# A decoder layer on one core: where the routed tiles' next rows are loaded and turned, and which buffers the shared down weights use

## Chip, cores and metric

The kernel runs on one core of one Trainium2 chip. The metric is device time in microseconds; the kernel before took 1041.7 us (median of three runs, 1040.75 to 1043.2).

## The reference

One decoder layer on `x` of 8 sequences of 112 tokens (896 tokens, width 512, fp32), each part with a layer norm ahead of it and a residual sum behind it: causal attention with 16 heads of 128; cross attention with 32 heads of 16 to a context of 375 rows per sequence; and a mixture of experts. All that the change touches is in the last part:

```python
probs = softmax(x @ gate_w.T)                      # 8 experts, the best 2 of each token
routing_weights, selected = top_k(probs, 2)        # normed to a sum of 1
out = (silu(x @ shared_gate.T) * (x @ shared_up.T)) @ shared_down.T          # 704 wide
y[e] = (silu(x @ expert_gate[e].T) * (x @ expert_up[e].T)) @ expert_down[e].T  # 352 wide
out = out + sum over the token's two experts of weight * y[e]
```

## The kernel before

The first two thirds of the kernel (attention and cross attention) are the same before and after. The expert part begins with the shared gate and up projections (`shared_chunk`, L645) and the routing (`route`). Routing gives every pair of token and expert a slot. The slots of one expert stand together, in units of 64 slots, and two units make a tile of 128 slots: 18 tiles (`NS`), 36 units. GpSimd scatters the normed token rows into `slots` in DRAM (L807).

**The routed loop** (L956) goes over tiles j = 0 to 17 and one round more, as a pipeline over three steps of three tiles. In round j:

- `fetch(j+1)` (L835 to L844): SyncE loads the next tile's 128 rows from `slots` into `xt` (two buffers). TensorE transposes them in four 128x128 blocks into PSUM (`xt_t`, L841), ScalarE copies these to `xT` (L843).
- `gate_up(j, ...)` (L868): gate and up of tile j, in two halves of two chunks each of the 512 inputs. The two units of a tile use the two halves of TensorE's columns: unit 0 reads its expert's weights in place from `wex` at a register's offset, unit 1 reads a copy (`second`), which VectorE makes (`copy_second`, L831). So each matmul is 128 rows by 64 columns, and two run side by side.
- Between the two halves, `turn_hidden` (L885) transposes the hidden rows of tile j-1 in three blocks (`h_t`, L889), and VectorE copies them to `hT` (L890, L891).
- `gated(gu)` (L878): ScalarE's Silu (L880) and VectorE's product (L882) make the hidden rows of tile j.
- `down(j-1, ...)` (L894): six matmuls per tile, again two side by side (`y`, L898), a copy by ScalarE (L902) and a write to `routed` in DRAM from SyncE (L903).
- `load_down(j+1)` (L846): SyncE loads the down weights of the next tile's two units, each 256 rows (`wed_a`) and 96 rows (`wed_b`) of 512.

**Buffers of the down weights** (L948 and L949): the pool `weights` has three buffers of four 128x512 slices, `thirds`. Three units hold slices 0 to 2 of one buffer each, a fourth unit is pieced together from slice 3 of all three. Even tiles use buffers 0 and 1, odd tiles buffer 2 and the pieced one. So the last tile, 17, reads slice 3 of buffers 0 and 1.

**After the loop**, `wsd0` and `wsd1`, three slices each of the shared down weights, are loaded into the same pool (L978 to L982). GpSimd gathers every token's two routed rows (`add_routed`, L909), and VectorE adds them to the residual (L915). `finish` (L917) multiplies the shared hidden rows by the shared down weights on TensorE (`ys`, L924), two token tiles at a time in four groups, VectorE adds (L930), SyncE writes out (L931).

What sets the order: each engine works through its own instructions in the order in which the scheduler of the tile framework put them, which is close to the order of the code but not the same. DMAs are started by the engine named in the code (`nc.sync`, `nc.scalar`, `nc.gpsimd`) when their turn comes there, and wait in that engine's order for what they depend on. A tile of a pool that takes the place of an older one waits until all reads of the older one, in whichever slice, are done.

Of the kernel before, what the change touches and what calls it, by code (L numbers as in the profile page):

```python
# [15 lines left out]
F32 = mybir.dt.float32  # L16
# [5 lines left out]
P = 128  # L22
B, S, D = 8, 112, 512
# [20 lines left out]
NS = (NU + 1) // 2  # L44
# [32 lines left out]
def decoder_layer(  # L77
    ctx: ExitStack, tc: tile.TileContext, x, ctxT, wqk, wv_all, wo, wx, wgate, wsgu, wsd, wegu, wed_a, wed_b, consts, out
):
    nc = tc.nc  # L80
# [6 lines left out]
    wpool = ctx.enter_context(tc.tile_pool(name="weights", bufs=3))  # L87
# [26 lines left out]
    slots = dpool.tile([NS * P, D], F32, name="slots")  # L114
    routed = dpool.tile([NS * P, D], F32, name="routed")

    def psum(pool, name):
        return pool.tile([P, 512], F32, tag=pool.name, name=name)
# [53 lines left out]
    with ExitStack() as sa:  # L172
# [106 lines left out]
        for g in range(NG):  # L279
# [11 lines left out]
            if g == 0:  # L291
                first_weights = load.ins
                with tc.issue_after(first_weights):
                    nc.sync.dma_start(out=gw, in_=wgate)
                    nc.sync.dma_start(
                        out=slots.rearrange("(j p) d -> p j d", p=P),
                        in_=zeros[:, None, :].to_broadcast([P, NS, D]),
# [326 lines left out]
    with ExitStack() as ff:  # L624
# [4 lines left out]
        tp = ff.enter_context(tc.tile_pool(name="slot", bufs=2))  # L629
# [194 lines left out]
        def second(j, c):  # L824
            return stand[(j * ND + c) % len(stand)]

        def copy_second(j, chunks):
            if j not in moved:
                moved[j] = nc.vector.value_load(expert[:1, 2 * j + 1 : 2 * j + 2], min_val=0, max_val=E - 1)
            for c in chunks:  # L830
                nc.vector.tensor_copy(  # L831
                    second(j, c), wex[:, bass.ds(moved[j], 1), c, :].rearrange("p o f -> p (o f)")
                )

        def fetch(j):  # L835

            xt = tp.tile([P, D], F32, tag="xt", name="xt")
            nc.sync.dma_start(out=xt, in_=slots[j * P : (j + 1) * P, :])
            pt = psum(mm, "xt_t")
            for c in range(ND):  # L840
                nc.tensor.transpose(pt[:, c * P : (c + 1) * P], xt[:, c * P : (c + 1) * P], ident)  # L841
            xT = tp.tile([P, ND, P], F32, tag="xT", name="xT")
            nc.scalar.copy(xT, pt.rearrange("p (c s) -> p c s", c=ND))  # L843
            return xT  # L844

        def load_down(j):  # L846

            wd = down_w[2 * (j % 2) : 2 * (j % 2) + 2]
            for u in range(2):
                e = nc.sync.value_load(expert[:1, 2 * j + u : 2 * j + u + 1], min_val=0, max_val=E - 1)  # L850
                if u == 0 or j % 2 == 0:
                    w = wd[u]
                    nc.sync.dma_start(out=w[:, 0:2, :], in_=wed_a[bass.ds(e, 1)].rearrange("o p c d -> (o p) c d"))
                    nc.sync.dma_start(
                        out=w[: FCH[2][1], 2, :], in_=wed_b[bass.ds(e, 1)].rearrange("o p d -> (o p) d")
                    )
                    wd[u] = [w[:, i, :] for i in range(3)]
                else:
                    for i in range(2):
                        nc.sync.dma_start(  # L860
                            out=wd[u][i], in_=wed_a[bass.ds(e, 1), :, i].rearrange("o p d -> (o p) d")
                        )
                    nc.sync.dma_start(
                        out=wd[u][2][: FCH[2][1]], in_=wed_b[bass.ds(e, 1)].rearrange("o p d -> (o p) d")
                    )
            return wd

        def gate_up(j, e, xT, gu, chunks):  # L868
            for c in chunks:
                for k in range(2):  # L870
                    cols = slice(k * FF, (k + 1) * FF)
                    for n, w in (
                        (halves[0], wex[:, bass.ds(e, 1), c, cols].rearrange("p o f -> p (o f)")),
                        (halves[1], second(j, c)[:, cols]),
                    ):
                        nc.tensor.matmul(gu[k][n, :FF], xT[:, c, n], w, start=(c == 0), stop=(c == ND - 1))  # L876

        def gated(gu):  # L878
            g = tp.tile([P, FF], F32, tag="sg", name="sg")
            nc.scalar.activation(g, gu[0][:, :FF], AF.Silu)  # L880
            h = tp.tile([P, FF], F32, tag="sh", name="sh")
            nc.vector.tensor_tensor(h, g, gu[1][:, :FF], ALU.mult)  # L882
            return h

        def turn_hidden(h):  # L885
            pt = psum(mm, "h_t")
            hT = tp.tile([P, 3, P], F32, tag="hT", name="hT")
            for i, (f0, fn) in enumerate(FCH):
                nc.tensor.transpose(pt[:fn, i * P : (i + 1) * P], h[:, f0 : f0 + fn], ident)  # L889
            nc.vector.tensor_copy(hT[:, :2, :], pt[:, : 2 * P].rearrange("p (c s) -> p c s", c=2))  # L890
            nc.vector.tensor_copy(hT[: FCH[2][1], 2, :], pt[: FCH[2][1], 2 * P : 3 * P])  # L891
            return hT

        def down(j, hT, wd):  # L894
            ps = psum(mm, "y")
            for i, (_, fn) in enumerate(FCH):
                for n, w in zip(halves, wd):
                    nc.tensor.matmul(  # L898
                        ps[n, :], hT[:fn, i, n], w[i][:fn], start=(i == 0), stop=(i == len(FCH) - 1)
                    )  # L900
            y = tp.tile([P, D], F32, tag="y", name="y")
            nc.scalar.copy(y, ps)  # L902
            nc.sync.dma_start(out=routed[j * P : (j + 1) * P, :], in_=y)  # L903
# [44 lines left out]
        thirds = [wpool.tile([P, 4, 512], F32, tag="w", name=f"wd{i}") for i in range(3)]  # L948
        down_w = [*thirds, [t[:, 3, :] for t in thirds]]  # L949
        moved = {}  # L950
        copy_second(0, (0, 1))
        ready = {0: fetch(0)}
        wds = {0: load_down(0)}
        copy_second(0, (2, 3))
        h = {}
        for j in range(NS + 1):  # L956
            if j + 1 < NS:
                ready[j + 1] = fetch(j + 1)
            if j < NS:
                gu = [psum(sc, "gate"), psum(sc, "up")]  # L960
                e = nc.tensor.value_load(expert[:1, 2 * j : 2 * j + 1], min_val=0, max_val=E - 1)
                gate_up(j, e, ready[j], gu, (0, 1))
            if j + 1 < NS:
                copy_second(j + 1, (0, 1))
            if j >= 1:
                hT = turn_hidden(h.pop(j - 1))
            if j < NS:
                gate_up(j, e, ready[j], gu, (2, 3))
                if j + 1 < NS:
                    copy_second(j + 1, (2,))  # L970
                h[j] = gated(gu)
                if j + 1 < NS:
                    copy_second(j + 1, (3,))
            if j >= 1:
                down(j - 1, hT, wds.pop(j - 1))
            if j + 1 < NS:
                wds[j + 1] = load_down(j + 1)
        wsd_t = []  # L978
        for i in range(2):
            w = wpool.tile([P, 4, 512], F32, tag="w", name=f"wsd{i}")  # L980
            nc.sync.dma_start(out=w[:, :3, :], in_=wsd[:, 3 * i : 3 * i + 3, :])
            wsd_t.append(w)  # L982
        pairs = ((0, 4), (1, 5), (2, 6), (3,))
        for tiles in pairs:
            for t in tiles:
# [79 lines left out]
```

## Time and profile before

| What | Value |
|---|---|
| median of three runs | 1041.7 us (1040.75 to 1043.2) |
| profiled execution: its own time, its span | 1046.2 us, 1044.4 us |
| mean granted TensorE clock in that span | 0.991 |
| routed loop, from its first transposes to the last `y` | about 839.9 to 999.8 us of the span |
| `gate` and `up` (L876), copies included | 144 + 144 matmuls each on `wex`, 459 to 471 ns |
| `y` (L898) | 216, 592 ns |
| turned rows `xt_t` (L841), hidden rows `h_t` (L889) | 72 and 54, 284 and 291 ns |
| `ys` (L924) | 84, 644 ns |
| loads of rows `xt` (SyncE) | 18 of 256 KB, 5.3 us to landing |
| loads of shared down weights (SyncE) | 2 of 768 KB, 4.4 and 6.3 us to landing |

Durations of single matmuls overlap, for they are pipelined: the distance of their starts is what a matmul costs. The chain of waits gives that better; its lines hold a start, a length, an engine, the name of what was written, the line of the kernel and a count. Every fp32 matmul appears as two records, and one in which two units run side by side as four.

### The profile page before, as it was taken

Reading aid. Unit: us, or ns where it says so; the run is one execution under the profiler, and the core shown is the slowest. Engines: PE = TensorE matmul, PEld = TensorE weight load, DVE = VectorE, ACT = ScalarE, POOL = GpSimd, SP = SyncE. Lnnn points to the kernel's source line nnn. Section 1 sums busy time; section 2 is a strip of 40 time slices with the busy share of each in tenths; the row PEclk is TensorE's granted clock in tenths of the full one; section 3 lists DMA queues with packets and bytes.
Section 4 is the critical chain, followed back from the end, with each engine's and each line's share of the span. In section 5 each row is a group of like instructions: output and inputs, shape, how many; then the busy total and the mean of one; then the engine's idle time right before and its main releaser. Section 6 shows DMA issues by size and latency. Waiting matters only on the chain.

```text
span 1044.4 us, 14683 instructions
## 1 busy us (share of the span) xinstructions
PE 1020.3 (98%) x5760; PEld 540.1 (52%) x5760; DVE 381.8 (37%) x744; ACT 277.4 (27%) x516; POOL 201.3 (19%) x223
## 2 busy tenths in 40 slices
PE   5999999999999999999999999999999989999988
PEld 3556555655565455645555555556665544444433
DVE  3345234522453244654223332242224133333223
ACT  2122011201120013123545554565532011111100
POOL 3241044103410221132100111011053200000041
PEclk9999999999999999999999999999989999999989
DMA  9421002101210120001000000001158247777664
GB/s 347 178 85 46 24 18 83 47 0 41 82 48 1 41 82 8 1 1 41 30 31 31 1 31 30 32 1 41 42 226 323 93 143 226 228 226 230 209 194 121
DMA packets 31092, 95.66 MB, mean 92 GB/s; under 512 B 3888, under 2 KB 5808, under 8 KB 27440
## 3 DMA queue, kind: packets, MB, share of 16 engines
q1 hardware_dynamic: 28272, 86.31, 24.7%
q0 software_dynamic: 2320, 7.63, 2.3%
q8 instruction: 46, 0.75, 0.3%
q10 hardware_dynamic: 432, 0.79, 0.2%
q14 instruction: 22, 0.18, 0.1%
HBM read 78.85 MB, written 14.94 MB: 90 GB/s over the span
## 4 chain that ended last, share of the span: by engine, by line
PE 92%; issue 3%; DVE 2%; DMA 2%; POOL 1%; ACT 0%; SPq 0%; DVEq 0%; POOLq 0%; ACTq 0%
PE qk L256 15%; PE o L343 9%; PE v L333 9%; PE xv L435 8%; PE k L423 8%; PE gu L645 6%; PE xs L511 5%; PE gate L876 4%; PE y L898 4%; PE pv L536 4%; PE up L876 4%; PE ys L924 4%; PE z L221 2%; PE s L186 2%; PE qk L311 1%
## 5 line engine op out<-in xcount | busy, mean ns | idle before, releaser
L519 ACT ACTIVATE e<-xs 125x448 f32<-125x448 f32 x192 | 88.9, 549 | 51.5 <-PE xs L511 51.3
L333 PE MATMUL v<-w,xn 128*128 128x512 f32 x224 | 100.4, 594 | 0.0
L343 PE MATMUL o<-wo,zT 128*128 128x512 f32 x224 | 99.9, 594 | 0.0
L435 PE MATMUL xv<-wx,ctx 128*125 128x512 f32 x192 | 88.4, 603 | 0.0
L423 PE MATMUL k<-wx,ctx 128*125 128x512 f32 x192 | 87.6, 601 | 0.0
L256 PE MATMUL qk<-xc,wc 128*128 128x448 f32 x180 | 70.1, 539 | 0.0
L645 PE MATMUL gu<-xn,sw 128*128 128x448 f32 x176 | 67.5, 540 | 0.0
L343 PEld LDWEIGHTS o<-wo,zT 128*128 128x128 f32 x224 | 41.0, 190 | 44.1 <-issue 44.0
L333 PEld LDWEIGHTS v<-w,xn 128*128 128x128 f32 x224 | 40.7, 190 | 42.1 <-issue 41.1
L407 POOL TENSOR_TENSOR sq<-kraw 125x512 f32<-125x512 f32 x24 | 25.2, 1050 | 184.9 <-ACT kraw L405 184.9
L511 PE MATMUL xs<-qT,kT 32*125 32x224 f32 x768 | 55.4, 380 | 1.0 <-ACT e L519 1.0
L876 PE MATMUL gate<-wex,xT 128*64 x144 | 56.0, 471 | 0.3 <-ACT xT L843 0.3
L423 PEld LDWEIGHTS k<-wx,ctx 128*125 128x125 f32 x192 | 34.3, 187 | 40.1 <-issue 40.1
L207 POOL TENSOR_TENSOR s<-s,sm 112x448 f32<-112x448 f32 x32 | 30.2, 943 | 128.9 <-DVE sm L206 101.3
L435 PEld LDWEIGHTS xv<-wx,ctx 128*125 128x125 f32 x192 | 34.1, 187 | 39.9 <-issue 39.9
L876 PE MATMUL up<-wex,xT 128*64 x144 | 54.4, 459 | 0.0
L511 PEld LDWEIGHTS xs<-qT,kT 32*125 32x125 f32 x768 | 36.6, 184 | 32.1 <-issue 27.6
L831 DVE COPY xn<-wex 128x704 f32 x60 | 31.2, 524 | 57.7 <-PE up L876 57.6
L909 POOL DMA_INDIRECT got<-routed,at x14 | 15.1, 1080 | 190.1 <-DMA routed<-y 186.1
L256 PEld LDWEIGHTS qk<-xc,wc 128*128 128x128 f32 x180 | 34.2, 190 | 33.5 <-issue 32.3
L256 PE MATMUL qk<-xn,w 128*128 128x448 f32 x120 | 50.2, 539 | 0.0
L898 PE MATMUL y<-wd,hT 128*64 128x512 f32 (+1 forms) x216 | 49.5, 592 | 0.6 <-ACT y L902 0.6
(181 smaller groups left out, 1475.2 us busy)
## 6 DMA issues: line engine op xcount, KB each, us to landing
wd<-in_wed_a SPq DMA_DIRECT2D x27, 512.0 KB, 3.7
wex<-in_wegu SPq DMA_DIRECT2D x8, 1408.0 KB, 17.0
wd<-in_wed_b SPq DMA_DIRECT2D x36, 192.0 KB, 4.5
w<-in_wqk SPq DMA_DIRECT2D x6, 1024.0 KB, 4.8
ctx<-in_ctxT SPq DMA_DIRECT2D x8, 750.0 KB, 4.2
slots<-zeros SPq DMA_DIRECT2D x1, 4608.0 KB
xt<-slots SPq DMA_DIRECT2D x18, 256.0 KB, 5.3
wd<-in_wed_a SPq DMA_DIRECT2D x18, 256.0 KB, 4.7
```

What stands on the lines that cost most here:

```text
L256: nc.tensor.matmul(ps[:, :HALF], wt[:, c * P : (c + 1) * P], x[:, c, :], start=(c == 0), stop=(c == 1))
L333: nc.tensor.matmul(ps, xn1[:, c, t * P : (t + 1) * P], wv[:, c, :], start=(c == 0), stop=(c == ND - 1))
L343: nc.tensor.matmul(ps, zT[:, h, t * P : (t + 1) * P], wog[:, h, :], start=(h == 0), stop=(h == GH - 1),)
L423: nc.tensor.matmul(ps[:MC, :], ctxs[b][:, c, m * MC : (m + 1) * MC], wxk[:, c, :], start=(c == 0), stop=(c == ND - 1),)
L435: nc.tensor.matmul(ps[:MC, :], ctxs[b][:, c, m * MC : (m + 1) * MC], wxv[:, c, :], start=(c == 0), stop=(c == ND - 1),)
L511: nc.tensor.matmul(strips[j][:MC, ci * 2 * S : (ci + 1) * 2 * S], keys[b][rows, 2 * cp + ci, m * MC : (m + 1) * MC], queries[b][rows, 2 * ...
L519: nc.scalar.activation(e[:, :, j, :, :].rearrange("p c e s -> p c (e s)"), strips[j][:MC, : 4 * S].rearrange("p (c f) -> p c f", c=2), AF.Exp,
L536: nc.tensor.matmul(ps[VW * j : VW * (j + 1), g * S : (g + 1) * S], v[:, m, 16 * cp + h, :], es[m][:, h // 8, (h % 8) // 2, h % 2, :], star ...
L645: nc.tensor.matmul(ps[:, :HALF], w[:, c, i % 2, k, :], xn3[:, c, cols], start=(c == 0), stop=(c == ND - 1))
L876: nc.tensor.matmul(gu[k][n, :FF], xT[:, c, n], w, start=(c == 0), stop=(c == ND - 1))
L898: nc.tensor.matmul(ps[n, :], hT[:fn, i, n], w[i][:fn], start=(i == 0), stop=(i == len(FCH) - 1))
L924: nc.tensor.matmul(p, hidden[n, i, t * P : (t + 1) * P], wsd_t[i // 3][n, i % 3, :], start=(i == 0), stop=(i == 5))
```

## The change

Three edits, all in the routed loop and just after it.

1. `fetch` is split. `rows_of(j)` only loads the rows, from SyncE for tiles 0 and 1 and from ScalarE's queue for the rest; the first two are loaded ahead of the loop. `turned_rows(j)` transposes and copies them and then starts the load of tile j+2.
2. In the loop, the next tile's rows are turned behind `turn_hidden` of the tile before, between the two halves of `gate_up`, and not at the head of the round.
3. The shared down weights are written to `thirds[0]` and `thirds[1]` themselves, slices 0 to 2, and not to new tiles of the pool.

```diff
-        def fetch(j):
-
+        def rows_of(j):
             xt = tp.tile([P, D], F32, tag="xt", name="xt")
-            nc.sync.dma_start(out=xt, in_=slots[j * P : (j + 1) * P, :])
+            (nc.sync if j < 2 else nc.scalar).dma_start(out=xt, in_=slots[j * P : (j + 1) * P, :])
+            return xt
+
+        def turned_rows(j):
+            xt = loaded.pop(j)
             pt = psum(mm, "xt_t")
             for c in range(ND):
                 nc.tensor.transpose(pt[:, c * P : (c + 1) * P], xt[:, c * P : (c + 1) * P], ident)
             xT = tp.tile([P, ND, P], F32, tag="xT", name="xT")
             nc.scalar.copy(xT, pt.rearrange("p (c s) -> p c s", c=ND))
+            if j + 2 < NS:
+                loaded[j + 2] = rows_of(j + 2)
             return xT
...
-        ready = {0: fetch(0)}
+        loaded = {j: rows_of(j) for j in range(2)}
+        ready = {0: turned_rows(0)}
...
         for j in range(NS + 1):
-            if j + 1 < NS:
-                ready[j + 1] = fetch(j + 1)
             if j < NS:
                 gu = [psum(sc, "gate"), psum(sc, "up")]
...
             if j >= 1:
                 hT = turn_hidden(h.pop(j - 1))
+            if j + 1 < NS:
+                ready[j + 1] = turned_rows(j + 1)
             if j < NS:
                 gate_up(j, e, ready[j], gu, (2, 3))
...
-        wsd_t = []
-        for i in range(2):
-            w = wpool.tile([P, 4, 512], F32, tag="w", name=f"wsd{i}")
+
+        wsd_t = thirds[:2]
+        for i, w in enumerate(wsd_t):
             nc.sync.dma_start(out=w[:, :3, :], in_=wsd[:, 3 * i : 3 * i + 3, :])
-            wsd_t.append(w)
```

## The prediction

> **What bounds the kernel now.** I read the busy shares first, then busy time by stretches, then the chain of waits through the routed stage, then SyncE's own timeline.
>
> ```profile
> PE 1020.3 (98%) x5760; PEld 540.1 (52%) x5760; DVE 381.8 (37%) x744; ACT 277.4 (27%) x516; POOL 201.3 (19%) x223
> ```
>
> TensorE is the bound: only the order and the gaps of its own work can matter. The stretches (length; busy time by engine; then granted clock, DMA share, GB/s) show where gaps are:
>
> ```profile
> 840.00:860.00 20.00, 17.36 (x108) 8.18 (x108) 7.10 (x17) 4.54 (x9) 0.00 (x0) 1.00 0.45 140
> 860.00:880.00 20.00, 20.00 (x123) 8.56 (x121) 7.60 (x18) 3.22 (x6) 0.00 (x0) 1.00 0.80 233
> 1000.00:1020.00 20.00, 17.43 (x35) 7.31 (x36) 7.60 (x12) 0.59 (x1) 12.32 (x12) 0.83 0.73 218
> ```
>
> Between the two gaps TensorE is never idle, so there only a shorter order of work can gain. In the last stretch the clock falls as well. The chain of waits (start, length, what) at the first gap, with SyncE's timeline below it:
>
> ```profile
> 840.07 0.45 PE xt_t L841 x4
> ...
> 842.63 6.35 DMA xt<-slots
> 848.98 0.14 issue
> 849.12 0.63 PE xt_t L841 x4
> ```
>
> ```profile
> 841.15 0.86 SPq L860 DMA_DIRECT2D wd<-in_wed_a  x2
> 842.19 0.33 SPq L863 DMA_DIRECT2D wd<-in_wed_b  x1
> 842.63 7.46 SPq L838 DMA_DIRECT2D xt<-slots  x3
> ```
>
> The rows of tile 2 are issued on SyncE behind the five down-weight loads of tile 1, land 6.35 us later, and TensorE stands in front of their transposes. The same chain at the last two tiles and the end:
>
> ```profile
> 979.30 0.59 PE xt_t L841 x4
> 979.88 0.74 PE gate L876 x4
> 980.62 0.59 PE up L876 x4
> ...
> 982.40 0.48 PE h_t L889 x3
> 982.88 0.74 PE gate L876 x4
> ...
> 985.39 2.58 PE y L898 x12
> 987.97 0.59 PE gate L876 x4
> ...
> 998.07 4.36 DMA wsd<-in_wsd
> 1002.43 0.14 issue
> 1002.57 38.14 PE ys L924 x84
> ```
>
> Read the gate groups: 0.74 us directly after transposes, 0.59 directly after the y matmuls (tile 17 has no next rows to turn). And 4 transposes take 0.45 after full-width matmuls (840.07) but 0.59 after y. Transposes are 128*128 in the groups of instructions; gate, up and y are 128*64. So entering and leaving a block of transposes costs about 0.15 us each way.
>
> **What the Trainium skill says.** "TensorEngine Tiling (Array Packing)", Key Properties: changing the tiling mode drains TensorE, changing only the tile does not. The trace agrees, at 0.15 us a change. "TensorE: Matmul & The Clock Gate", Part 1: an idle window of about 3.4 us halves the clock, a busy one of about 3.4 us restores it, and the windows run freely. The trace agrees: full until about 1001.9, 0.50 until about 1008.7, after a gap from about 999.7 to 1002.57; a gap of similar length at 846 did not drop it, so phase counts. "DMA: Bandwidth & Descriptors", Issuing engines are not separate DMA queues: another issuing queue saves issue time, not bandwidth. The trace of before has no row load on ScalarE; its x loads there took 1.38 us for three, 0.46 each.
>
> **The change, part by part.**
>
> *Rows turned behind the hidden rows.* Per tile before: turned rows 0.59, gate and up 0.74+3x0.59=2.51, hidden 0.48, gate and up 2.51, y 2.58: 8.67 us, which is the distance of the chain's tiles (979.30 to 987.97). After: gate and up follow y, 4x0.59=2.36; then 7 transposes at 0.11 (0.45/4) with one entry, 0.92; gate and up 2.51; y 2.58: 8.37. Saved 0.30. The built order on TensorE has hidden and row transposes adjacent in tiles 1 to 16. Tile 1 is in the next term, so 15x0.30 = **4.5 us**. What was covered stays covered: Silu of a tile starts 6.2 us before its hidden transposes (976.18 to 982.33), and needs itself (0.46) and the product (0.52): 5.2 us spare, 4.4 once the transposes come 0.7 sooner. The copy of the turned rows (0.59) then has 5.1 us of gate, up and y in front of its reader. Waits of TensorE on itself, new in the built order, are for work two tiles back: zero.
>
> *Rows loaded from ScalarE.* 16 issues of about 0.46 us move there: ScalarE has per tile 0.59+0.46+0.59 of 8.4 us, so it has room. Behind each issue stand Silu and the y copy. Its waits are an older row load and one weight load issued about a tile (8 us) earlier; those land in 3.5 to 6.2 us (trace, weight tiles), so no hold. SyncE loses the same issues; its weight loads gain 0.4 us they don't need. For tile 2 the issue moves from 842.63 to about 841.7 (behind the copy and one Silu, both in the trace), no longer behind 1.4 MB in its own queue; even at 6.35 us it lands at 848.1. The reader moves too. After 841.23: half of gate and up with an exit 2.51, two transposes of tile 1 that the built order splits off (0.15+0.22), 2.51, 2.36, then hidden 0.48: rows of tile 2 are wanted at about 849.5. So the gap goes; next late is nothing, with 1.4 us spare. From 841.23 to the end of y of tile 0 before: 857.83, 16.6 us; after 2.51+0.37+2.51+2.36+0.92+2.51+2.58 = 13.8. Gain **2.8 us** (bounds: 1.3 if the load took 8 us and more, 3.2 if the split transposes are free).
>
> *Shared down weights in the units' buffers.* Before, the load waits at 998.07 for y of tile 17, whose second unit used the fourth slice of the same buffer. After, it writes only slices 0 to 2, last read by y of tile 16, which ends at 995.97. Issue about 996.0, ahead of that tile's routed write. At 4.36+0.14 it lands at 1000.5, at the 6.3 us of the second load at 1002.3. y of tile 17 ends near 999.7. TensorE starts ys at 1000.5 instead of 1002.57: **2.1 us** (0.3 to 2.8). The second load, issued at about 997, is needed 5 us into ys: covered. The gap shrinks to 0.8 us, so no window is mostly idle and the half clock from 1002.57 to 1008.7 goes: half of 6.1, **3.0 us**. Bounds: 0 if ordinary runs don't drop there, 6 if they drop at 846 too; I take what the trace shows. Next late would be the gathers: VectorE's last routed add is at 1026.96, so the bank for the last ys tile is free at 1028.4; TensorE wants it at 1000.5+3x9.8 = 1029.9. 1.5 us spare.
>
> **Sum**: 4.5+2.8+2.1+3.0 = 12.4. The profiled execution took 1046.2 (span 1044.4): 1033.8. The shown runs have a median of 1041.7; the profiled one also had a clock of 0.83 at 740 to 760 (3.4 us) that the change doesn't touch. Taken from the median: **1029.3**.
>
> **Rivals.** *Shared weights land late*: 6.3 us in place of 4.5, for two 768 KB loads now overlap; the gap stays and so does the half clock. Gain 4.5+2.8+0.3=7.6: 1034.1. For: the second load took that long. Against: it ran beside other traffic, and the first is ahead in the queue. *The merge saves nothing*: the 0.15 belongs to each group of transposes, whatever stands before. Gain 7.9: 1033.8. Against: 0.45 for four behind full-width matmuls. *More*: ordinary runs also pay a half clock after the gap at 846; 15.4: 1026.3. *Slower*: a row load on ScalarE waits for its semaphore's older weight load and holds Silu, product, hidden transposes. The hold begins 1.4 us before Silu could start, so 1.4+4.4 = 5.8 us are free; past that each us costs 15, and it decides from 5.8+12.4/15 = 6.6 us. At 7 us: 18-12.4, 1047.3. Against: it needs loads that take 15 us. That the order isn't as meant is excluded by the built order.
>
> **Chances.** All parts as summed 0.63 (1027.5 to 1031.5), late weights 0.12, no merge 0.10, more 0.09, slower 0.06. 1026 to 1034.5 holds the first four nearly whole. About 0.2% can be told from no change: faster 0.91, same 0.03 (late weights and no merge and a smaller first gain together), slower 0.06.
>
> **What would show it.** Right: tiles 8.37 us apart in the chain, hidden and row transposes as one block near 0.92; no wait on row loads at 846; ys starting about 0.8 us after y of tile 17, clock 1.00 throughout. Wrong: Silu starting over 5 us later relative to its gate matmuls; a wait of TensorE on the shared weights over 2 us with the clock at 0.50; a wait of ys on VectorE near its fourth pair.

## The result and the profile after

The changed kernel took 1031.1 us (median of six runs, 1029.8 to 1034.9), beside 1041.2 for the kernel before on the same chip: a ratio of 0.9906, with a 95% interval from 0.9881 to 0.9932. That is 10.1 us less, or 7 to 12.4 by the interval; forecast were 12.4. The profiled execution of the changed kernel took 1034.9 us, with a span of 1033.1.

The busy time by stretch, for the three windows that the prediction showed and the one from 980 (the columns are busy us of TensorE, its weight loads, VectorE, ScalarE and GpSimd, then granted clock, DMA share and GB/s):

```profile
840.00:860.00 20.00, 19.49 (x125) 9.33 (x125) 9.22 (x21) 4.55 (x9) 0.00 (x0) 1.00 0.58 166
860.00:880.00 20.00, 20.00 (x124) 8.95 (x122) 7.68 (x17) 3.73 (x7) 0.00 (x0) 1.00 0.81 244
980.00:1000.00 20.00, 18.43 (x84) 7.57 (x81) 1.76 (x5) 2.22 (x4) 0.05 (x1) 1.00 0.59 191
1000.00:1020.00 20.00, 20.00 (x50) 8.12 (x49) 10.34 (x16) 0.00 (x0) 13.81 (x14) 1.00 0.69 198
```

TensorE's busy time in the first stretch rose from 17.36 to 19.49 us, and in the last it is 20.00 at a clock of 1.00, where it was 17.43 at 0.83. ys now starts before 1000, so what is left of its wait, 1.0 us, lies in the third row (the other 0.6 us that TensorE is idle there, it waits for a copy of y, as before). The chain of waits where the first gap was (start, length, what):

```profile
844.55 0.37 PE xt_t L844 x2
844.91 0.74 PE gate L881 x4
...
849.80 0.48 PE h_t L894 x3
850.28 0.44 PE xt_t L844 x4
850.71 0.74 PE gate L881 x4
...
853.23 2.58 PE y L903 x12
855.81 0.59 PE gate L881 x4
```

No load of rows stands in the chain any more. Hidden and row transposes are one block of 0.48 and 0.44 us (a transpose leaves one record, so these are three and four of them), gate behind y costs 0.59, gate behind the block 0.74. The same chain at the last two tiles and the end:

```profile
978.88 2.58 PE y L903 x12
981.46 0.59 PE gate L881 x4
...
986.82 2.58 PE y L903 x12
989.40 0.02 PE h_t L894
989.42 4.68 DMA wd<-in_wsd
994.11 0.14 issue
994.24 35.12 PE ys L929 x84
```

The shared weights are issued when y of tile 16 ends (989.40), and ys takes 35.12 us in place of 38.14.

So that the start of the routed stretch, which moves with the first two thirds of the kernel, doesn't enter, all times below run from the first row transposes (840.79 here, 840.07 before). From the starts and lengths of the chain, in us:

| Stretch | before | after | gain | forecast |
|---|---|---|---|---|
| first row transposes to the end of the first y | 17.76 | 15.02 | 2.74 | 2.8 |
| to the end of y of tile 16 (16 tiles) | 138.14 | 133.59 | 4.55 | 4.5 |
| to the start of ys | 6.60 | 4.84 | 1.76 | 2.1 |
| ys | 38.14 | 35.12 | 3.02 | 3.0 |
| first row transposes to the end of the span | 204.33 | 192.31 | 12.02 | 12.4 |

In the pair of profiled executions every term stands within 0.35 us of its forecast. The medians are 2 us closer than that, and this difference is what most of the experiments are about.

### The profile page after: what moved, and what is told of

It reads as the page before. It is cut to its first block, busy times and chain, and to the rows that moved or that the text cites. A ratio compares the mean times of both kernels' runs of the same rounds, so it can differ in the third digit from the quotient of the medians.

```text
span 1033.1 us, 14696 instructions
## 1 busy us (share of the span) xinstructions
PE 1012.6 (98%) x5760; PEld 540.4 (52%) x5760; DVE 381.8 (37%) x744; ACT 277.6 (27%) x516; POOL 199.8 (19%) x223
## 4 chain that ended last, share of the span: by engine, by line
PE 92%; issue 3%; DMA 2%; DVE 1%; POOL 1%; ACT 0%; SPq 0%; DVEq 0%; POOLq 0%; ACTq 0%
PE qk L256 15%; PE o L343 9%; PE v L333 9%; PE xv L435 8%; PE k L423 8%; PE gu L645 6%; PE xs L511 5%; PE gate L881 4%; PE y L903 4%; PE up L881 4%; PE pv L536 4%; PE ys L929 3%; PE z L221 2%; PE s L186 2%; PE qk L311 1%
```

## The experiments

The theory at their start: the four terms as summed, and 10.1 in place of 12.4 because the profiled execution of before isn't like the others of before. The rival: the terms hold in every execution, and something upstream of the routed tiles hides them.

**The merge of the transposes, taken apart.** In the changed kernel, the next rows are turned between chunks 2 and 3:

```diff
-            if j + 1 < NS:
-                ready[j + 1] = turned_rows(j + 1)
             if j < NS:
-                gate_up(j, e, ready[j], gu, (2, 3))
+                gate_up(j, e, ready[j], gu, (2,))
+            if j + 1 < NS:
+                ready[j + 1] = turned_rows(j + 1)
+            if j < NS:
+                gate_up(j, e, ready[j], gu, (3,))
```

> The changed kernel, but the next rows are turned between chunks 2 and 3 of gate and up, so not next to the hidden rows. Theory (what saves is that two blocks of full-width transposes stand together and share one entry and one exit): tiles 8.67 us apart in place of 8.37, 15 to 16 times 0.30 us, so 4.5 to 4.8 us longer than the changed kernel. Rival (what saves is that the turn has left the head of the round, behind y): tiles stay 8.37 to 8.4 us apart, and the time is that of the changed kernel.

Measured: 1035.8 us, 0.9943 of the kernel before (0.9920 to 0.9966). The stretch from the first row transposes to the end is 197.2 us, 4.9 longer than the changed kernel's. Its chain of waits:

```profile
967.32 0.48 PE h_t L894 x3
967.79 0.74 PE gate L881 x4
968.53 0.59 PE up L881 x4
969.13 0.59 PE xt_t L844 x4
969.71 0.74 PE gate L881 x4
```

Each of the two blocks has its own exit again (two gate groups of 0.74), the row transposes pay their entry (0.59 for 0.44), and the starts of y (971.05 and 979.73) are 8.68 us apart. The merge is what saves, and leaving the head of the round is not. (The medians on the same chip are only 2.5 us apart, 1035.8 and 1033.3; they hold half clock ahead of the routed stage, which the stretch leaves out.)

**Order and early issue without ScalarE's queue.** The rows are turned where the change turns them, the first two tiles' rows are loaded ahead of the loop, but from SyncE, and the third edit is left out:

```diff
-            (nc.sync if j < 2 else nc.scalar).dma_start(out=xt, in_=slots[j * P : (j + 1) * P, :])
+            nc.sync.dma_start(out=xt, in_=slots[j * P : (j + 1) * P, :])
```

> The kernel before with the rows turned behind the hidden rows and the first two row loads ahead of the loop, but every row load on SyncE, and without the third edit. Theory of the sum (order and early issue save, the queue does not): tiles 8.37 us apart, no wait in front of the rows of tile 2, the stretch from the first routed transposes to the end 7 us shorter than before (204.3), so about 197; time 6 to 8 us below the kernel before. Rival (ScalarE's queue removes the wait for tile 2): tiles 8.37 apart, but TensorE waits 2 to 3 us for the rows of tile 2, and the gain is 4.5 us.

Measured: 1036.4 us, 0.9945 (0.9926 to 0.9965), so 5.3 us less than before by the medians, under the 6 to 8 expected, which the interval (3.6 to 7.7) still allows in part. The first row transposes to the end of the first y take 15.02 us, exactly what they take in the changed kernel. TensorE's waits from there to the end:

```profile
PE ys L929 <- DMA wsd<-in_wsd: 2.6, 1, 2.6
PE y L903 <- ACT y L907: 0.6, 1, 0.6
PE gate L881 <- ACT xT L846: 0.5, 1, 0.5
```

No wait on rows is in it, for any of the 18 tiles: the 2.8 us came without ScalarE's queue. The stretch was 195.6 us, below the 197 expected, because ys lost less to the clock (36.81 us, not 38.14).

**Row loads early, rows turned at the head.** This is the other half: loads as in the change, the turn left where it was, the third edit left out.

```diff
         for j in range(NS + 1):
             if j + 1 < NS:
-                ready[j + 1] = fetch(j + 1)
+                ready[j + 1] = turned_rows(j + 1)
```

> The kernel before with the row loads as in the change (two ahead of the loop, the rest on ScalarE's queue as soon as the rows two tiles back are turned), but the rows are still turned at the head of the round, and the third edit is left out. Theory of the sum (this alone removes the wait for the rows of tile 2): tiles stay 8.67 us apart, TensorE doesn't wait for rows, and the stretch from the first routed transposes to the end of the first y is 2 to 3 us shorter than the 17.76 of before; time 1 to 3 us below the kernel before. Rival (the reader of the rows has to move too, for at the head of the round it comes too soon after the issue): TensorE still waits over 1 us for the rows of tile 2, and the gain is under 1.5 us.

Measured: 1040.8 us, 0.9981 (0.9960 to 1.0003). The first of its waits of TensorE that bear on this:

```profile
PE xt_t L844 <- DMA xt<-slots: 0.8, 1, 0.8
```

The load for tile 2 is issued at 836.58 and lands 5.89 us later, still 0.8 us after its transposes stand in front of TensorE. The same stretch is 16.13 us, 1.1 more than after. This lies between the two: the wait is below the rival's 1 us, but it isn't gone, and the stretch is 1.6 us below the 17.76 of the profile that the prediction read. That profile is not a like one, though: two profiles below with the old loads, whose stretch also begins early (at 835.24 in "Work in the wait" and at 835.92 in the third of the kernel before), wait 0.9 and 1.1 us and take 16.34 and 16.48 us. Beside them the early loads alone gain 0.2 to 0.35 us, which one profile can't tell from nothing; the reader has to move.

**The third edit alone.** The kernel before with

```diff
-        wsd_t = []
-        for i in range(2):
-            w = wpool.tile([P, 4, 512], F32, tag="w", name=f"wsd{i}")
+        wsd_t = thirds[:2]
+        for i, w in enumerate(wsd_t):
             nc.sync.dma_start(out=w[:, :3, :], in_=wsd[:, 3 * i : 3 * i + 3, :])
-            wsd_t.append(w)
```

> The kernel before with the third edit alone (shared down weights into the units' buffers). Theory of the sum: ys starts about 1.8 us sooner after the y of tile 16 (4.8 for 6.6 us) in every execution, and the clock stays at 1.00 in ys, which gives 3.0 us more only in executions in which the kernel before drops there: 2 to 5 us faster by the medians, tiles still 8.67 us apart. Rival (the clock has nothing to do with the wait): 1.8 us faster and no more, ys as long as before (38 us). Rival (weights land late once SyncE carries the row loads too): under 1 us faster, ys 38 us.

Measured: 1039.5 us, 0.9974 (0.9960 to 0.9988), so 2.7 us less (1.3 to 4.2). The end of its chain of waits:

```profile
993.02 2.60 PE y L898 x12
995.62 4.79 DMA wd<-in_wsd
1000.42 0.14 issue
1000.55 35.12 PE ys L924 x84
```

ys starts 4.93 us behind y of tile 16 and runs at full clock, as in the changed kernel. That is the theory's profile. The time allows at most 4.2 us, though, where 1.7 and 3.0 would be 4.7.

**Work in the wait.** The kernel before with three matmuls ahead of ys, whose result nobody uses. In the built order one of them stands ahead of y of tile 17 and two behind it.

```diff
+        fill = psum(sc, "fill")
+        for i in range(3):
+            nc.tensor.matmul(fill, hidden[:, i, :P], hidden[:, i, :512], start=(i == 0), stop=(i == 2))
```

> The kernel before with three full-width matmuls added ahead of ys, whose result nobody uses: TensorE has some work in the wait for the shared weights, which land no sooner. Theory of the clock (the wait of 2.85 us causes the half clock): ys about 35.1 us in place of 38.1 with the clock at 1.00, although it starts no sooner (up to 0.4 us later); up to 2.7 us faster. Rival (the drop comes from the long run before and not from the wait): ys still 38 us, and the time the same or 0.3 us longer.

Measured: 1042.8 us, 0.9999 (0.9985 to 1.0014). Waits and chain of its profile:

```profile
PE ys L924 <- DMA wsd<-in_wsd: 0.8, 1, 0.8
```

```profile
992.08 4.23 DMA wsd<-in_wsd
996.31 0.14 issue
996.45 35.12 PE ys L924 x84
```

The weights land no sooner (ys starts 6.78 us behind y of tile 16, for 6.60), but TensorE idles 0.8 us and not 2.8, and ys runs at full clock. This supports the wait as the cause of the half clock. Yet the time doesn't move: a gain of 2.7 us lies outside the interval (at most 1.6). So over all executions the half clock can't be worth 3.0 net of what follows it.

**The changed kernel again.** No edit.

> The changed kernel itself, for more executions of it. Theory (the stretch from the first routed transposes to the end became 12.0 us shorter in the profiles, and the rest of the difference is the start of that stretch, which moves by some 5 us from execution to execution in both kernels): with more executions the gain goes to 11 to 12.5 us, and a second profile has again some 192.3 us from the first routed transposes to the end. Rival (part of the gain is given back in executions that aren't profiled, because the kernel before pays the half clock ahead of ys in few of them): the gain stays at 10 us.

Measured: 1033.3 us (1029.3 to 1034.3), 0.9908 (0.9880 to 0.9936) of 1041.8. Its profile has 192.33 us from the first row transposes to the end and 35.12 us of ys, like the first one, though it began 4.0 us earlier (836.77). The gain stays near 10 us, as the rival had it; whether for its reason, the next profiles show.

**The kernel before, four more profiles.** No edit. The first went with 21 more executions, the others are single executions.

> The kernel before itself, for the granted clock and span of each execution. Theory (the medians differ by 10.1 us and not by 12.4 because the half clock ahead of ys falls into some executions only): the times follow the mean clock, some near 1039.5 with a clock near 0.995 and some near 1043 to 1046 with a clock near 0.991. Rival (every execution pays the drop ahead of ys, and the sum is short elsewhere): the profile of this second look shows 38.1 us of ys again, and the mean clock of the shortest executions is no higher than 0.994. No difference in the medians, whichever holds.

> The kernel before, one more profile, to see what an execution that isn't the longest spends in the stretch from the first routed transposes to the end (204.3 and 204.2 us in the two profiles so far). Theory that the half clock ahead of ys was sized too large: ys at full clock, 35.1 to 36.8 us, stretch 201 to 203. Theory that the first gap was sized too large: the rows of tile 2 land in about 5 us in place of 6.35, stretch about 203. Rival (the stretch is always 204 and only its start moves): 204.0 to 204.5 again.

> The same kernel and the same question as the profile ahead of it: half clock smaller than summed (ys 35.1 to 36.8 us, stretch 201 to 203), first gap smaller than summed (rows of tile 2 in about 5 us, stretch about 203), or a stretch of 204.0 to 204.5 again.

> The same kernel and the same question once more: half clock smaller than summed (ys 35.1 to 36.8 us, stretch 201 to 203), first gap smaller than summed (rows of tile 2 in about 5 us, stretch about 203), or a stretch of 204.0 to 204.5 again.

Measured: the 22 executions took 1038.7 to 1045.6 us, with a median of 1041.9. Their mean clocks go from 0.991 to 0.998, and those near 1039 and 1040 have 0.996 to 0.998, so neither of the two bounds set for them (0.995 and 0.994) holds. But none has 1.000, which 4 of the 12 executions of the changed kernel have: the kernel before ran some stretch at half clock each time, here or upstream. The profiles, worked out as the table above (us; the first column is the profile that the prediction read):

| | predicted from | 1st | 2nd | 3rd | 4th | after, both |
|---|---|---|---|---|---|---|
| first row transposes begin at | 840.07 | 836.71 | 839.81 | 835.92 | 840.15 | 840.79, 836.77 |
| to the end of the first y | 17.76 | 19.12 | 17.23 | 16.48 | 17.51 | 15.02 |
| y of tile 16 to ys | 6.60 | 6.59 | 6.44 | 6.39 | 6.58 | 4.84, 4.86 |
| ys | 38.14 | 36.66 | 36.85 | 36.87 | 36.60 | 35.12 |
| to the end of the span | 204.33 | 204.19 | 202.39 | 201.58 | 202.55 | 192.31, 192.33 |

Two terms shrink. In the last three, ys lost 1.5 to 1.75 us to the clock and not 3.0. By windows of one us, the kernel before as the prediction read it:

```profile
1001.00:1002.00 1.00, 0.00 (x0) 0.00 (x0) 0.00 (x0) 0.00 (x0) 0.00 (x0) 0.92 0.97 395
1002.00:1003.00 1.00, 0.43 (x1) 0.46 (x2) 0.00 (x0) 0.00 (x0) 0.00 (x0) 0.50 0.94 207
...
1005.00:1006.00 1.00, 1.00 (x2) 0.34 (x1) 0.00 (x0) 0.00 (x0) 0.69 (x2) 0.50 0.59 238
...
1007.00:1008.00 1.00, 1.00 (x3) 0.48 (x2) 0.00 (x0) 0.00 (x0) 0.86 (x1) 0.50 0.58 143
1008.00:1009.00 1.00, 1.00 (x3) 0.35 (x2) 0.61 (x1) 0.00 (x0) 0.84 (x1) 0.67 0.77 221
```

and the fourth profile:

```profile
1001.00:1002.00 1.00, 0.00 (x0) 0.00 (x0) 0.00 (x0) 0.00 (x0) 0.00 (x0) 0.98 0.95 377
1002.00:1003.00 1.00, 0.62 (x1) 0.50 (x2) 0.00 (x0) 0.00 (x0) 0.00 (x0) 0.50 0.92 231
...
1005.00:1006.00 1.00, 1.00 (x3) 0.53 (x2) 0.00 (x0) 0.00 (x0) 0.69 (x2) 0.82 0.62 156
1006.00:1007.00 1.00, 1.00 (x4) 0.44 (x3) 0.00 (x0) 0.00 (x0) 0.70 (x2) 1.00 0.68 236
```

Read the clock column, third from the right. A window at 0.92 was at full clock for 0.84 of its us, so the drop lasts from 1001.84 to 1008.66, 6.8 us, in one and from 1001.96 to 1005.36, 3.4 us, in the other. So the rival that the gain stays near 10 us was right on the size and not on the reason: a half clock stands behind one of the two gaps in each of the five profiles, but mostly for half as long. And the rows of tile 2 landed in 5.07 to 6.10 us where the prediction's profile had 6.35, so in the last three the first gap was 1.5 to 2.5 us long over what the change leaves, not 2.74.

The first of the four is another case. Its waits of TensorE:

```profile
PE ys L924 <- DMA wsd<-in_wsd: 2.8, 1, 2.8
PE xt_t L841 <- DMA xt<-slots: 2.1, 1, 2.1
PE ys L924 <- DVE x L930: 1.3, 1, 1.3
```

Here the clock halved behind the first gap (845.94 to 849.34, which is why the first row is 19.12) and stayed full in ys. But at full clock ys then waited 1.3 us for VectorE's adds, which stand behind the gathers. So in this profile the wait for the adds took back what the full clock gave. That isn't so in every execution: in "Work in the wait", with ys as late as here, ys took 35.12 us without that wait. The 14 gathers were started within 16.4 us there and within 19.5 us here.

**Where the windows fall.** The clock and TensorE's busy time in narrow windows also say which gap an execution pays for. In each profile the half clock begins and ends on a grid of 3.41 us: in the one that the prediction read at 752.66, 759.49, 762.90, 766.32, 1001.84 and 1008.66, and the 235.52 us from the fourth to the fifth are 69 times 3.413. The table has TensorE's idle time in the window of that grid in which it was idle longest, and the clock in the window behind it:

| Profile | at the first gap | ahead of ys | in the window after a drop |
|---|---|---|---|
| predicted from | 1.47 us, full | 2.08 us, half | 0.73 us, half again |
| 1st | 2.05 us, half | 1.77 us, full | 0.00 us, full |
| 2nd | 1.46 us, full | 2.61 us, half | 0.04 us, full |
| 3rd | 1.07 us, full | 2.60 us, half | 0.00 us, full |
| 4th | 1.50 us, full | 2.36 us, half | 0.43 us, full |
| after, both | 0.51 us, full | 1.00 and 0.78 us, full | no drop |

At these two places the clock halved behind 2.05 us of idle time and more, and stayed full behind 1.77 and less. The seven other profiles of this document fit (up to 1.41 us: full; 2.36 and 2.56 us: half). So the same wait of 2.6 to 2.8 us ahead of ys costs no window, one or two, by where the grid cuts it, and the 1.0 us that the change leaves lies below the 1.77 us wherever it falls. A second window followed behind 0.73 us of idle time, and none behind 0.43 and less. That is an account of these two places, not of the clock in general: at 750 to 766 us, where cross attention works in matmuls of 32 rows or columns, the profile that the prediction read dropped behind windows with 0.33 and 0.67 us of idle time.

**A version without the rest of the wait.** The shared weights in slices, in the changed kernel:

```diff
         for i, w in enumerate(wsd_t):
-            nc.sync.dma_start(out=w[:, :3, :], in_=wsd[:, 3 * i : 3 * i + 3, :])
+            for c in range(3):
+                nc.sync.dma_start(out=w[:, c, :], in_=wsd[:, 3 * i + c, :])
```

> The changed kernel with the shared down weights in six loads of 256 KB in place of two of 768 KB. Theory (what is left of the wait ahead of ys, 1.9 us on the chain, is the size of the first load, which ys needs one slice at a time): the first slice lands in 2 to 3 us, ys starts behind the y of tile 17 without a wait, and the time is 1 to 1.9 us below the changed kernel's, some 11 to 12 us below the kernel before. Rival (six issues on SyncE and shared bandwidth delay the later slices): ys waits for its second or fourth slice instead, and the time is the changed kernel's or up to 1 us longer.

Measured: 1030.6 us, 0.9901 (0.9878 to 0.9925). ys begins 3.7 us behind y of tile 16, with no wait for weights in it, 1.1 us sooner than in the changed kernel. The size of the loads isn't all that changed: the first three slices are issued at 983.36, 1.75 us before y of tile 16 ends, where the changed kernel issues its first load at that end. But its waits of TensorE now have

```profile
PE ys L929 <- DVE x L920: 1.2, 1, 1.2
```

and the stretch to the end is 193.0 us, 0.7 longer than the changed kernel's. Neither of the two theories had this: the wait went from the weights to VectorE's gather adds.

To that, the output of two token tiles written directly behind their gathers, which changes the built order of VectorE's adds:

```diff
         for tiles in pairs:
             for t in tiles:
                 add_routed(t, at, share)
-        for tiles in pairs:
             finish(tiles)
```

> The changed kernel with the shared down weights in six loads, as before, and with the output of two token tiles written in the code directly behind their two gathers, which puts VectorE's adds of the first two ys tiles behind the fifth gather add and not between the fifth and the tenth. Theory (with the slices the wait for weights went, and a wait of 1.2 us for VectorE's adds took its place): ys runs without a wait, 35.1 us, and the stretch from the first routed transposes to the end is 190.4 to 191.2 us, 1.1 to 1.9 below the changed kernel's 192.3. Rival (the gathers themselves are the limit, not the order of the adds): the wait for VectorE stays, and the stretch is 192 to 193 us.

Measured: 1030.1 us, 0.9892 (0.9866 to 0.9919), with

```profile
PE ys L929 <- DVE x L935: 0.7, 1, 0.7
```

and 192.3 us to the end. The rival was right on the number: the third ys pair no longer waits, the last tile's ys waits 0.7 us, because its bank comes free behind the adds of the second pair, and these stand in VectorE's order behind the last gather add. Both versions are level with the changed kernel in what the intervals can tell.

## Why the prediction was right, term by term

- **Rows turned behind the hidden rows, 4.5 us: right.** 4.55 in the profile, and 4.9 come back when the two blocks of transposes are parted. The rival that the merge saves nothing is refuted.
- **First gap, 2.8 us: right for the profile it was read from, too large for others.** 2.74 there, 1.46 to 2.5 against the last three profiles of before (2.05 on average). The reason given was half right. The issue from ScalarE came at 841.74, as forecast, but the order with two loads ahead of the loop, all on SyncE's queue, reached the same 15.02 us. What removes the gap is the later reader together with the earlier issue, not the queue. The later reader might do alone: with the old issue the rows landed at most 8.91 us behind the first row transposes (848.98 less 840.07), and the new order reads them 9.49 us behind (850.28 less 840.79). This is an estimate; it was not run.
- **Earlier shared weights, 2.1 us: slightly large.** 1.76: the 768 KB landed in 4.68 us, not in 4.36. The rival that they land in 6.3 us is refuted.
- **Half clock goes, 3.0 us: the mis-sized term.** The mechanism held: with 1.0 us of wait in place of 2.8 the clock stayed at 1.00 in both profiles. The size did not. The prediction's words were "I take what the trace shows", with bounds from 0 to 6, and it took the term from an execution of 1046.2 us and subtracted it from a median of 1041.7. That execution had a drop of 6.8 us. Three others had 3.4 us, worth 1.5 to 1.75 us (36.60 to 36.87 less 35.12), and one had its drop at the first gap and paid 1.5 us in ys, most of it for VectorE's adds. What the Trainium skill, "TensorE: Matmul & The Clock Gate", Part 1, says of windows of about 3.4 us fits: the drops are one such window (3.4 us) or two (6.8 us). The prediction says after it that an idle window halves the clock and that the trace agrees; measured, 2.05 us of idle time in a window of 3.41 were enough. Three profiles are few for an average: the mean clock of whole executions rose from 0.9944 (59 of the kernel before) to 0.9969 (22 with the third edit alone), an estimate of 2.5 us less lost to the clock, upstream included. So the term was too large for most executions, and its average stays open between 1.65 and 3.0.
- **The sum.** With the averages of the last three profiles: 4.5+2.05+1.63+1.65 = 9.8 us (their stretches average 202.2, less 192.3: 9.9). The medians gave 10.1 and, in the second comparison, 8.4 (ratios 0.9906 and 0.9908). With one window in place of two, and the average gap, the sum meets the measurement. That 1031.1 fell inside the narrower range of the prediction (1027.5 to 1031.5) is in part luck: it is 1.8 us above the forecast 1029.3, and the second comparison's 1033.3 lies outside that range. The changed kernel's executions with a mean clock of 1.000 took 1029.3 to 1030.3 us, the others 1030.9 to 1034.9, and in both of its profiles the half clock lies wholly ahead of the routed stage.
- **The slower rival is refuted.** Silu waits for its gate matmuls and for nothing else, in 18 tiles, as this line of ScalarE's waits in the changed kernel says (us in total, times, longest):

```profile
ACT sg L885 <- PE gate L881: 26.2, 18, 4.1
```

- **"More", a half clock at both gaps, was not seen.** Of five profiles of before, one dropped at the first gap and four at the last, none at both. That no execution does isn't shown.
- The 1.5 us that the prediction gave the gathers as spare were too much: taking away 1.1 us more, by slices, ran into their adds for 1.2 us, and at the third group of ys and not at the last.

What stays open: how often an execution loses one window, two or none, and why the clock drops at 750 to 766 us. With all loads on SyncE the 16 tiles took 133.64 us, beside 133.59 in the changed kernel, so the merged order didn't need ScalarE's queue; together with the third edit that was not run.

## What to carry to other kernels

Price a half clock from several profiled executions, or lay the grid of its windows over the gap: here the same 2.6 to 2.8 us of waiting cost none, one or two windows of 3.41 us, and gaps with at most 1.77 us in one window cost none. Look also at what stands behind it: in one profile VectorE's adds took back the gain. On TensorE, put blocks of full-width transposes side by side when the matmuls around them are narrower: here each block that no longer stands alone was worth 0.30 us, at no cost to its readers. Where a load is late for its reader, look at moving the reader too: here a later reader with an earlier issue removed the gap whichever queue issued the load, and the earlier issue alone left a wait of 0.8 us.

## What was not expected of the hardware

- The same load of 256 KB, issued from the same queue at the same place of the program, landed in 5.07 to 6.35 us over five executions.
- The first row transposes began anywhere from 835.1 to 840.8 us in kernels whose code up to there doesn't differ in what TensorE does. The start goes with the half clock at 750 to 767 us: 10.2 us of it in the profiles that begin at 839.6 to 840.8, 6.8 in those at 836.7 and 836.8, and 3.4 or none in those up to 836.4. Such a spread of 5.7 us covers terms of 2 us in single times; stretches inside the span are free of it.
- Six issues in place of two on SyncE cost nothing that the profile shows: three of 256 KB took 1.57 us to issue, and ys waited for none of the slices.
